# First x loaded by two queues, its statistics raised to the power by halves, and the taps' loads issued by ScalarE

## The chip, the cores and the metric

The kernel runs on one core of a Trainium2 chip. The metric is device time in microseconds (us), the median of the runs of one program. The engines are PE (TensorE: matmuls, with PEld for its weight loads), DVE (VectorE), ACT (ScalarE), POOL (GpSimd) and SP (SyncE, which here only issues transfers). Each engine works through its own instructions in order; a transfer (DMA) is issued by SP, ACT or POOL as one of these instructions and then runs beside them.

## The reference

Two graph layers over 128 graphs of 128 nodes with 256 channels, in float32. Layer 0 is a message-passing layer with a convolution and a GRU; layer 1 is a set of graph convolutions over fixed groups of nodes. Both work on the normalized x:

```python
h = jnp.maximum(_layernorm(x, axis=-1), 0.0)
x = x + _L0_gnn_ref(h, adj, ...)
h = jnp.maximum(_layernorm(x, axis=-1), 0.0)
x = x + _L1_gnn_ref(h, adj, ...)
```

What the change touches is the beginning of layer 0, where `_layernorm(x)` is (x - mean) / sqrt(var + eps) and the convolution branch is:

```python
xc = jnp.transpose(x, (0, 2, 1))
h = _bn(_conv1d(xc, conv1_w, 0), bn1_g, bn1_b, bn1_m, bn1_v)   # 1 tap
h = jax.nn.relu(h)
h = _bn(_conv1d(h, conv2_w, 8), bn2_g, bn2_b, bn2_m, bn2_v)    # 17 taps
x_conv = jnp.transpose(jax.nn.relu(h + xc), (0, 2, 1))
```

`_bn` multiplies by scale = g / sqrt(v + eps) and adds b - m * scale.

## The kernel before

**Tiling.** The 128 graphs are worked in 32 groups q of four graphs, and these in two batches of 16 groups. A group's x is a tile `xa` of 128 partitions by four blocks of 256 channels (512 KB). `load_x` (L385) loads it in four pieces j, one graph each, of 32 partitions and 128 KB; every group's statistics need all four. Four buffers of `xa` are in rotation, so group q uses the buffer of group q - 4, which is free once that one's transposes are done.

**Stage a** (L395), once per group: statistics of the four blocks on DVE (`moments`, L268: bn_stats and bn_aggr for each, then one add of eps), the power -0.5 on POOL (L277, constant `mhalf` out of the tile `cst`), normalizing on DVE (L282), transposes on PE into `ph` (L418), relu on ACT into `hTa` (L420), a store of `hTa` to `hTd` by POOL (L423), the one-tap convolution as matmuls `pc` with `c1w` (L429), the add of the row `brow` on DVE (L432), relu on ACT (L434), and matmuls `pf` that take the result into a Fourier basis (L444), copied into X by DVE and ACT (L450, L452). `hTa` has two buffers: group q waits until the store of group q - 2 has been read out.

**Taps.** The 17-tap convolution is a product in the Fourier basis, so its weights are transformed once, beside stage a: `tap_weights` (L477) goes through four loads n of eight steps m. `load_taps` (L468) brings one load `wt` (two buffers) in five transfers: r = 0 to 3, 256 KB each into 16 partitions, by the issuers passed to it in turn, and the 17th tap (`wt[16::32]`, 64 KB into four partitions) by the first of them. A step is eight matmul instructions `pw` (L496) into four PSUM tiles, three from a pool of three banks (`pgat`) and one from a pool of five (`ptmp`); the copies `ws` (L501 on ACT, L503 on DVE) empty them, ACT two at even m and three at odd m; POOL stores `ws` to `wfd` (L508). Load 0 is issued in `fold`, load 1 before step (n, m) = (0, 3), load 2 before (1, 0) and load 3 before (2, 0). `load_late` (L254) brings three constants (`fus`, `wse`, the rest of `cst`) at step (1, 3).

**The beginning.** `fold` (L285) folds the batch norms: eps is added to both variances on DVE (L292), POOL raises them to -0.5 (L293), `moments` of group 0 follow, then scale and shift of bn1 and bn2, three DVE operations each (L297 to L299). ACT spreads the four columns of bn1's scale and shift into `wide` (L304), PE turns them into rows `prow` (L305), DVE multiplies `c1w` by the scale row (L309) and ACT copies the shift row to `brow` (L310). `normalize` of group 0 stands before that, `brz` (a sum of two GRU biases, needed much later) between.

**Order.** Nothing is reordered after the program text: the generators of the stages are merged by a planner (`Order`, L179) with written costs and due times, which fixes each engine's list. The change leaves costs and due times as they are. At the top, ACT issues the first part of `cst` and `vec` (the bias and batch-norm vectors); SP issues x of group 0, `c1w`, x of groups 1 and 2 (L1235 to L1238), then `fold` runs.

Of the kernel before, what the change touches and what calls it, by code (L numbers as in the profile page):

```python
# [11 lines left out]
ALU = mybir.AluOpType  # L12
# [6 lines left out]
EPS = 1e-5  # L19
# [22 lines left out]
WIDE = 32  # L42
# [104 lines left out]
CFIRST = CAT["tap"][1]  # L147
# [63 lines left out]
def kernel(ctx: ExitStack, tc: tile.TileContext, x, adj, consts, vecs, w_se, conv1_w,  # L211
                    conv2_w, w_msg, b_msg, w_ih, w_hh, W1, W2, b2, fusion_w, out):
    nc = tc.nc
# [16 lines left out]


    cst = cp.tile([P, CONSTS.shape[1]], FP, name="cst")
    nc.scalar.dma_start(out=cst[:, :CFIRST], in_=consts[:, :CFIRST])
    vec = cp.tile([P, NVEC], FP, name="vec")
    nc.scalar.dma_start(out=vec, in_=vecs)

    def c(name):
        a, b = CAT[name]
        return cst[:, a:b]

    def v(name, i=None):
        a, b = VAT[name]
        return vec[:, a:b] if i is None else vec[:, a + i:a + i + 1]
# [10 lines left out]
    def load_late():  # L254

        nc.sync.dma_start(out=fus, in_=fusion_w.partition_broadcast(P))
        nc.sync.dma_start(out=wse, in_=w_se.rearrange("(k p) o -> p k o", p=P))
        nc.sync.dma_start(out=cst[:, CFIRST:], in_=consts[:, CFIRST:])
# [4 lines left out]
    brz = cp.tile([P, 4], FP, name="brz")  # L263
# [4 lines left out]
    def moments(src, tag):  # L268

        st = f2.tile([P, 4, 6], FP, tag=tag + "st", name="st", bufs=4)  # L270
        mv = f2.tile([P, 4, 2], FP, tag=tag + "mv", name="mv", bufs=4)
        rs = f2.tile([P, 4], FP, tag=tag + "rs", name="rs", bufs=4)
        for t in range(4):
            nc.vector.bn_stats(st[:, t], src[:, t])
            nc.vector.bn_aggr(mv[:, t], st[:, t])
        nc.vector.tensor_scalar(rs, mv[:, :, 1], EPS, None, op0=ALU.add)
        nc.gpsimd.tensor_tensor(rs, rs, c("mhalf")[:, :4], ALU.pow)  # L277
        return mv, rs

    def normalize(dst, src, mv, rs):  # L280
        for t in range(4):
            nc.vector.tensor_scalar(dst[:, t], src[:, t], mv[:, t, 0:1], rs[:, t:t + 1],  # L282
                                    op0=ALU.subtract, op1=ALU.mult)

    def fold():  # L285


        s = cp.tile([P, 4], FP, name="s_bn")
        t = cp.tile([P, 4], FP, name="t_bn")
        for i, bn in enumerate(("bn1", "bn2")):  # L290
            scl[bn], sft[bn] = s[:, 2 * i:2 * i + 2], t[:, 2 * i:2 * i + 2]
            nc.vector.tensor_scalar(scl[bn], v(bn + "_v"), EPS, None, op0=ALU.add)  # L292
        nc.gpsimd.tensor_tensor(s, s, c("mhalf")[:, :4], ALU.pow)  # L293
        MOM[0] = moments(XA[0], "a")
        load_taps(0, nc.gpsimd, nc.sync)
        for bn in ("bn1", "bn2"):
            nc.vector.tensor_mul(scl[bn], scl[bn], v(bn + "_g"))  # L297
            nc.vector.tensor_mul(sft[bn], v(bn + "_m"), scl[bn])
            nc.vector.tensor_sub(sft[bn], v(bn + "_b"), sft[bn])  # L299
        prow = ptmp.tile([P, 4, P], FP, tag="tmp", name="prow")  # L300
        wide = tw.tile([P, 4, P], FP, tag="wide", name="wide", bufs=1)
        for i, a in enumerate((scl["bn1"][:, 0:1], scl["bn1"][:, 1:2], sft["bn1"][:, 0:1],
                               sft["bn1"][:, 1:2])):
            nc.scalar.activation(wide[:, i], a.to_broadcast([P, P]), AF.Copy)  # L304
            nc.tensor.matmul(prow[:, i], wide[:, i], ident, start=True, stop=True)  # L305
        normalize(XA[0], XA[0], *MOM[0])
        nc.vector.tensor_add(brz, v("b_ih")[:, 0:4], v("b_hh")[:, 0:4])
        for k in range(2):
            nc.vector.tensor_mul(c1w[:, k], c1w[:, k], prow[:, 0:2].rearrange("p a c -> p (a c)"))  # L309
        nc.scalar.activation(brow, prow[:, 2:4].rearrange("p a c -> p (a c)"), AF.Copy)  # L310

    def fold_gates():

# [61 lines left out]
    LATE, XA, MOM = {}, {}, {}  # L375
# [8 lines left out]

    def load_x(t, q):  # L385
        for j in range(GB):
            nc.sync.dma_start(out=t[j * WIDE:(j + 1) * WIDE],
                              in_=x[q * GB + j].rearrange("(t n) c -> n t c", n=WIDE))

    def load_xa(q):  # L390
        if q not in XA:
            XA[q] = LATE["ab"].tile([P, 4, D], FP, tag="xa", name=f"xa{q}", bufs=4)
            load_x(XA[q], q)
# [74 lines left out]
    def load_taps(n, *engines):  # L468

        wt = tw.tile([P, 16, D], FP, tag="wt", name=f"wt{n}")  # L470
        src = conv2_w.rearrange("(r n i) t o -> n t r i o", r=4, n=4)[n]
        for r in range(4):
            engines[r % len(engines)].dma_start(out=wt[32 * r:32 * r + 16], in_=src[:16, r])
        engines[0].dma_start(out=wt[16::32], in_=src[16])
        wts.append(wt)

    def tap_weights():  # L477

        yield 0.0, 16.0
        for n in range(4):  # L480
            for m in range(8):
                if m == (0 if n else 3) and n < 3:
                    load_taps(n + 1, nc.sync, nc.gpsimd)
                if (n, m) == (1, 3):
                    load_late()
                if (n, m) == (2, 3):
                    nc.scalar.dma_start(out=ad0, in_=adj[:GB].rearrange("b n m -> n b m"))
                    nc.scalar.dma_start(out=bm0, in_=b_msg.partition_broadcast(P))
                if m % 2 == 0:
                    ws = tws[(0, 2, 1)[(4 * n + m // 2) % 3]].tile([P, 4, 4, D], FP, tag="ws",  # L490
                                                                   name=f"ws{n}_{m}")
                pws = [(pgat if r < 3 else ptmp).tile([P, 2, D], FP, tag="gat" if r < 3 else "tmp",
                                                      name=f"pw{n}_{m}_{r}") for r in range(4)]
                for r in range(4):
                    rows = slice(32 * r, 32 * r + TAPS)
                    nc.tensor.matmul(pws[r][:F], c("tap")[rows], wts[n][rows, 2 * m:2 * m + 2],  # L496
                                     start=True, stop=True)
                i = m % 2 * 2
                for r in range(4):
                    if r < 2 or (r == 2 and m % 2):  # L500
                        nc.scalar.activation(ws[:F, r, i:i + 2], pws[r][:F], AF.Copy)  # L501
                    else:
                        nc.vector.tensor_copy(ws[:F, r, i:i + 2], pws[r][:F])  # L503
                yield 0.9, 2.2
                if m % 2:
                    for r in range(4):
                        i0 = 64 * r + 16 * n + 2 * (m - 1)
                        nc.gpsimd.dma_start(out=wfd[:, i0:i0 + 4], in_=ws[:F, r])  # L508
        yield from fold_embedding()
        mid.close()  # L510
        wg = ctx.enter_context(tc.tile_pool(name="wg", bufs=1, reuse_waits="tile"))
        LATE["wrz"] = wg.tile([P, 7, 3, D], FP, name="wrz")
        LATE["wn"] = wg.tile([P, 7, 2, P], FP, name="wn")
        LATE["wh"] = wg.tile([P, 8, 1, P], FP, name="wh")[:, :7]
        LATE["io"] = near.enter_context(tc.tile_pool(name="io", bufs=2, reuse_waits="tile"))
        LATE["xe"] = near.enter_context(tc.tile_pool(name="xe", bufs=1, reuse_waits="tile"))
        LATE["fr"] = near.enter_context(tc.tile_pool(name="fr", bufs=1, reuse_waits="tile"))
        load_h(0)
        LATE["wmsg"] = LATE["fr"].tile([P, 2, D], FP, name="wmsg")
        LATE["bmsg"] = LATE["fr"].tile([P, D], FP, name="bmsg")  # L520
        nc.sync.dma_start(out=LATE["wmsg"], in_=w_msg.rearrange("(k p) o -> p k o", p=P))
        nc.sync.dma_start(out=LATE["bmsg"], in_=b_msg.partition_broadcast(P))
        EN[0] = load_n(0)
# [73 lines left out]
    def load_h(q):  # L597
        HT[q] = LATE["io"].tile([P, 2, 512], FP, tag="hT", name=f"hT{q}")
        nc.sync.dma_start(out=HT[q], in_=hTd[q])

    def load_n(q):
        if q not in HT:
            load_h(q)
        hT = HT.pop(q)
        if q:
            ad = LATE["io"].tile([P, GB, N], FP, tag="adj", name=f"adj{q}")
            nc.sync.dma_start(out=ad, in_=adj[q * GB:(q + 1) * GB].rearrange("b n m -> n b m"))
        return hT, ad if q else ad0
# [624 lines left out]
    order = Order()  # L1233
    take_turn("ab", 2)
    load_xa(0)  # L1235
    nc.sync.dma_start(out=c1w, in_=conv1_w.rearrange("(k p) o -> p k o", p=P))
    load_xa(1)
    load_xa(2)  # L1238
# [68 lines left out]
```

## Time and profile before

| | us |
|---|---|
| median of 3 runs | 1963.19 |
| lowest and highest run | 1960.7, 1964.54 |
| the profiled execution | 1960.66 |
| its span, first to last instruction | 1958.9 |
| PE busy in the span | 1925.5 (98%) |
| DVE, ACT, POOL busy | 1341.2, 670.8, 656.7 |
| share of the chain that ended last: PE, DVE, DMA | 83%, 11%, 2% |

Stage a of the first batch fills the first 155 us, with the taps beside it. In the first 49 us PE is busy for 44.66, in the next 49 for 48.96, in the third 49 for 47.33. The granted clock is 1.00 in all three, and the DMA engines' mean busy share 1.05, 1.03 and 0.89.

A row of the timeline is: start, duration, engine, line, operation, out<-in, count, and in brackets how long the engine stood idle before it and what ended that. The row of a transfer is the issuing instruction's alone ("SPq" and "ACTq" are these engines' own queues); when it landed is seen only by who waited for it. A row of the chain is start, duration and what the end of the kernel hung on in that time.

### The profile page before, as it was taken

The numbers are of one execution on the slowest core, as the hardware profiler recorded it, in microseconds if no ns is written. First come the engines' busy times: TensorE is split into PE (matmuls) and PEld (weight loads), VectorE is DVE, ScalarE is ACT, GpSimd is POOL, SyncE is SP. The second block draws the span as 40 slices with busy tenths as digits, with TensorE's granted clock in tenths as the row PEclk, the third lists the DMA queues.
The fourth block names the chain that finished last, engine by engine and source line by source line (L and its number), as shares of the span: only waits on it lengthen the run. The fifth ranks groups of instructions, "written<-read, shape, count | busy, mean of one in ns | idle before, by whom it ended". The sixth has DMA issues, their size and how long they took to land.

```text
span 1958.9 us, 32171 instructions
## 1 busy us (share of the span) xinstructions
PE 1925.5 (98%) x12048; PEld 1591.1 (81%) x12048; DVE 1341.2 (68%) x2965; ACT 670.8 (34%) x1504; POOL 656.7 (34%) x899
## 2 busy tenths in 40 slices
PE   9999999999999999999999999999999999999997
PEld 6668888889888888887888787888877788887865
DVE  6775445786443576796883886885788787588852
ACT  4664222445223334322223332232332223223233
POOL 3452666332565201332321333231133222114220
PEclk9999999999999999999999999999999999999999
DMA  9988878744778744633433344254344334334232
GB/s 217 308 276 271 272 252 286 218 142 172 251 255 260 213 114 132 188 95 84 112 95 97 96 108 112 79 134 97 92 115 101 89 101 112 100 90 120 63 70 68
DMA packets 180982, 296.66 MB, mean 151 GB/s; under 512 B 28326, under 2 KB 131947, under 8 KB 180571
## 3 DMA queue, kind: packets, MB, share of 16 engines
q1 hardware_dynamic: 134874, 162.20, 28.9%
q0 software_dynamic: 44800, 131.66, 23.8%
q8 instruction: 95, 1.56, 0.3%
q10 hardware_dynamic: 1152, 0.74, 0.1%
q14 instruction: 61, 0.49, 0.1%
HBM read 197.97 MB, written 109.05 MB: 157 GB/s over the span
## 4 chain that ended last, share of the span: by engine, by line
PE 83%; DVE 11%; DMA 2%; ACT 1%; issue 1%; SPq 1%; POOL 0%; DVEq 0%; ACTq 0%; POOLq 0%
PE p L776 37%; PE pa L550 7%; PE pm L663 5%; PE pz L1150 5%; PE ph L1138 5%; PE pc L429 4%; PE pb L550 3%; PE pf L444 3%; PE px L689 3%; PE pi L733 2%; PE pw L496 1%; DMA xa<-in_x 1%; PE ph L418 1%; PE py L1122 1%; DVE xc L742 1%
## 5 line engine op out<-in xcount | busy, mean ns | idle before, releaser
L958 POOL DMA_DIRECT2D x1d<-xt x128 | 101.2, 815 | 403.6 <-DVE xt L956 390.5
L582 DVE SCALAR_TENSOR_TENSOR y<-pa,kk 128x512 f32<-128x512 f32 x78 | 53.8, 690 | 151.4 <-ACT kk L581 151.4
L858 POOL DMA_DIRECT2D xt<-in_x x128 | 100.6, 793 | 161.3 <-DMA x1d<-xt 148.1
L550 PE MATMUL pa<-wf,X 128*128 128x256 f32 x640 | 152.2, 381 | 0.0
L776 PE MATMUL p<-th,wrz 128*128 128x256 f32 x512 | 134.2, 384 | 0.0
L776 PE MATMUL p<-tm,wrz 128*128 128x256 f32 x512 | 131.4, 379 | 0.0
L776 PE MATMUL p<-tc,wrz 128*128 128x256 f32 x512 | 131.4, 379 | 0.0
L550 PEld LDWEIGHTS pa<-wf,X 128*128 128x128 f32 x640 | 118.1, 190 | 16.2 <-issue 2.0
L429 PE MATMUL pc<-c1w,hTa 128*128 128x256 f32 x512 | 120.9, 382 | 2.8 <-DVE X L450 1.7
L663 PE MATMUL pm<-wmsg,hT 128*128 128x256 f32 x512 | 121.5, 382 | 0.0
L776 PEld LDWEIGHTS p<-th,wrz 128*128 128x128 f32 x512 | 94.7, 190 | 19.1 <-issue 6.6
L429 PEld LDWEIGHTS pc<-c1w,hTa 128*128 128x128 f32 x512 | 93.6, 190 | 20.1 <-DVE h L432 4.8
L776 PEld LDWEIGHTS p<-tc,wrz 128*128 128x128 f32 x512 | 97.2, 190 | 13.5 <-issue 0.5
L663 PEld LDWEIGHTS pm<-wmsg,hT 128*128 128x128 f32 x512 | 95.8, 190 | 15.2 <-ACT kk L581 1.4
L776 PEld LDWEIGHTS p<-tm,wrz 128*128 128x128 f32 x512 | 97.3, 190 | 13.2
L745 ACT ACTIVATE xc<-xc,t_bn 128x256 f32<-128x256 f32 x128 | 58.1, 501 | 145.3 <-DVE xc L742 145.3
L776 PE MATMUL p<-hTc,wrz 128*128 128x256 f32 x384 | 99.7, 382 | 1.3 <-DVE z L850 1.2
L776 PE MATMUL p<-xc,wrz 128*128 128x256 f32 x384 | 98.6, 379 | 0.0
L776 PE MATMUL p<-xm,wrz 128*128 128x256 f32 x384 | 98.5, 379 | 0.0
L545 POOL TENSOR_TENSOR wf<-wf 128x512 f32<-128x512 f32 x78 | 98.5, 1263 | 0.0
L1138 PE MATMUL ph<-yz,w 128*128 128x400 f32 (+3 forms) x448 | 96.6, 369 | 1.8 <-DVE yz L1125 1.8
L1150 PE MATMUL pz<-hz,w 128*128 128x400 f32 (+3 forms) x448 | 95.7, 368 | 0.5 <-DVE yz L1152 0.5
(213 smaller groups left out, 4329.5 us busy)
## 6 DMA issues: line engine op xcount, KB each, us to landing
wf<-wfd SPq DMA_DIRECT2D x160, 256.0 KB
wfd<-ws POOLq DMA_DIRECT2D x64, 320.0 KB, 9.3
yd<-y POOLq DMA_DIRECT2D x80, 256.0 KB, 4.4
yt<-yd SPq DMA_DIRECT2D x64, 320.0 KB
xa<-in_x SPq DMA_DIRECT2D x128, 128.0 KB
hTd<-hTa POOLq DMA_DIRECT2D x32, 512.0 KB, 6.5
hT<-hTd SPq DMA_DIRECT2D x32, 512.0 KB
xmd<-xnmp POOLq DMA_DIRECT2D x32, 512.0 KB, 6.0
```

The lines of the kernel that those rows point to most:

```text
L429: nc.tensor.matmul(pc[:, i], hT[:, k, (2 * h + i) * N:(2 * h + i + 1) * N], c1w[:, k], start=(k == 0), stop=(k == 1))
L444: nc.tensor.matmul(pf[:, i, :F * NB], h1[:, 2 * h + i, k * P:(k + 1) * P], fwd, start=True, stop=True)
L545: nc.gpsimd.tensor_tensor(WF[f][:, :, 2], WF[f][:, :, 0], WF[f][:, :, 1], ALU.add)
L550: nc.tensor.matmul(ps, xk(k), WF[f][:, k, s], start=(k == 0), stop=(k == 1))
L663: nc.tensor.matmul(pm[:, i], hT[:, k, j * N:(j + 1) * N], LATE["wmsg"][:, k], start=(k == 0), stop=(k == 1))
L689: nc.tensor.matmul(px[:, dc, i], msgs[h][:, i, dc * P:(dc + 1) * P], aT[:, 2 * h + i], start=True, stop=True)
L745: nc.scalar.activation(xc[:, co, s], xc[:, co, s], AF.Relu, bias=sft["bn2"][:, co:co + 1])
L776: nc.tensor.matmul(ps[:, m], w[:, i, k, m * P:(m + 1) * P], factor(i, x, t), start=first and j == 0, stop=last and j == len(n) - 1, skip_g ...
L858: nc.gpsimd.dma_start(out=xt[a * WIDE:(a + 1) * WIDE].rearrange("p b d c -> p (b d) c"), in_=slices(x[q * GB:(q + 1) * GB])[a])
L958: nc.gpsimd.dma_start(out=slices(x1d[q])[a], in_=xt[a * WIDE:(a + 1) * WIDE].rearrange("p b d c -> p (b d) c"))
L1138: nc.tensor.matmul(ph, w1[:, k, m * P:(m + 1) * P], yz[:, k, s:s + nb, o:o + n], start=(k == 0), stop=(k == 1))
L1150: nc.tensor.matmul(pz, w2[:, g, m, cc * P:(cc + 1) * P], hs[i][:, m], start=(m == 0), stop=(m == 3))
```

## The change

- `cst` and `vec` are no longer issued first by ACT. Pieces 1 and 3 of group 0's x go to ACT, pieces 0 and 2 stay on SP; `cst` follows on ACT, `vec` on SP ahead of `c1w`.
- The moments of group 0 are taken in two halves of two blocks, each with its own add of eps on DVE and its own power on POOL.
- bn2's scale and shift and `brz` come after `c1w` and `brow` instead of before.
- Taps load 0 was issued by POOL (r = 0, 2 and the 17th tap) and SP (r = 1, 3); now by ACT and SP. Loads 1 to 3 were issued by SP (r = 0, 2, 17th tap) and POOL; now by ACT and POOL.

```diff
--- before.py
+++ after.py
@@ -230,9 +230,7 @@
 
 
     cst = cp.tile([P, CONSTS.shape[1]], FP, name="cst")
-    nc.scalar.dma_start(out=cst[:, :CFIRST], in_=consts[:, :CFIRST])
     vec = cp.tile([P, NVEC], FP, name="vec")
-    nc.scalar.dma_start(out=vec, in_=vecs)
 
     def c(name):
         a, b = CAT[name]
@@ -270,11 +268,12 @@
         st = f2.tile([P, 4, 6], FP, tag=tag + "st", name="st", bufs=4)
         mv = f2.tile([P, 4, 2], FP, tag=tag + "mv", name="mv", bufs=4)
         rs = f2.tile([P, 4], FP, tag=tag + "rs", name="rs", bufs=4)
-        for t in range(4):
-            nc.vector.bn_stats(st[:, t], src[:, t])
-            nc.vector.bn_aggr(mv[:, t], st[:, t])
-        nc.vector.tensor_scalar(rs, mv[:, :, 1], EPS, None, op0=ALU.add)
-        nc.gpsimd.tensor_tensor(rs, rs, c("mhalf")[:, :4], ALU.pow)
+        for s in (slice(0, 4),) if src is not XA.get(0) else (slice(0, 2), slice(2, 4)):
+            for t in range(s.start, s.stop):
+                nc.vector.bn_stats(st[:, t], src[:, t])
+                nc.vector.bn_aggr(mv[:, t], st[:, t])
+            nc.vector.tensor_scalar(rs[:, s], mv[:, s, 1], EPS, None, op0=ALU.add)
+            nc.gpsimd.tensor_tensor(rs[:, s], rs[:, s], c("mhalf")[:, s], ALU.pow)
         return mv, rs
 
     def normalize(dst, src, mv, rs):
@@ -292,11 +291,14 @@
             nc.vector.tensor_scalar(scl[bn], v(bn + "_v"), EPS, None, op0=ALU.add)
         nc.gpsimd.tensor_tensor(s, s, c("mhalf")[:, :4], ALU.pow)
         MOM[0] = moments(XA[0], "a")
-        load_taps(0, nc.gpsimd, nc.sync)
-        for bn in ("bn1", "bn2"):
+        load_taps(0, nc.scalar, nc.sync)
+
+        def shift(bn):
             nc.vector.tensor_mul(scl[bn], scl[bn], v(bn + "_g"))
             nc.vector.tensor_mul(sft[bn], v(bn + "_m"), scl[bn])
             nc.vector.tensor_sub(sft[bn], v(bn + "_b"), sft[bn])
+
+        shift("bn1")
         prow = ptmp.tile([P, 4, P], FP, tag="tmp", name="prow")
         wide = tw.tile([P, 4, P], FP, tag="wide", name="wide", bufs=1)
         for i, a in enumerate((scl["bn1"][:, 0:1], scl["bn1"][:, 1:2], sft["bn1"][:, 0:1],
@@ -304,10 +306,11 @@
             nc.scalar.activation(wide[:, i], a.to_broadcast([P, P]), AF.Copy)
             nc.tensor.matmul(prow[:, i], wide[:, i], ident, start=True, stop=True)
         normalize(XA[0], XA[0], *MOM[0])
-        nc.vector.tensor_add(brz, v("b_ih")[:, 0:4], v("b_hh")[:, 0:4])
         for k in range(2):
             nc.vector.tensor_mul(c1w[:, k], c1w[:, k], prow[:, 0:2].rearrange("p a c -> p (a c)"))
         nc.scalar.activation(brow, prow[:, 2:4].rearrange("p a c -> p (a c)"), AF.Copy)
+        shift("bn2")
+        nc.vector.tensor_add(brz, v("b_ih")[:, 0:4], v("b_hh")[:, 0:4])
 
     def fold_gates():
 
@@ -384,7 +387,7 @@
 
     def load_x(t, q):
         for j in range(GB):
-            nc.sync.dma_start(out=t[j * WIDE:(j + 1) * WIDE],
+            (nc.scalar if q == 0 and j % 2 else nc.sync).dma_start(out=t[j * WIDE:(j + 1) * WIDE],
                               in_=x[q * GB + j].rearrange("(t n) c -> n t c", n=WIDE))
 
     def load_xa(q):
@@ -480,7 +483,7 @@
         for n in range(4):
             for m in range(8):
                 if m == (0 if n else 3) and n < 3:
-                    load_taps(n + 1, nc.sync, nc.gpsimd)
+                    load_taps(n + 1, nc.scalar, nc.gpsimd)
                 if (n, m) == (1, 3):
                     load_late()
                 if (n, m) == (2, 3):
@@ -1233,6 +1236,8 @@
     order = Order()
     take_turn("ab", 2)
     load_xa(0)
+    nc.scalar.dma_start(out=cst[:, :CFIRST], in_=consts[:, :CFIRST])
+    nc.sync.dma_start(out=vec, in_=vecs)
     nc.sync.dma_start(out=c1w, in_=conv1_w.rearrange("(k p) o -> p k o", p=P))
     load_xa(1)
     load_xa(2)
```

## The prediction

> **What bounds the kernel now.** I read the page first: PE is busy for 98% of the span, so a change elsewhere counts only where PE stands still for want of it. The chain of waits in order of time says where that is in the part the change touches (start, length, what):
>
> ```profile
> 2.10 3.71 DMA xa<-in_x
> 8.44 1.02 POOL rs L277
> 14.07 1.00 POOL rs L277
> 15.07 12.31 DMA hTd<-hTa
> 28.14 2.05 PE pc L429 x8
> ...
> 98.43 11.71 DMA xa<-in_x
> 113.04 1.99 PE pc L429 x8
> ```
>
> Before 28 us and around 110 us the chain runs through transfers; between and after, it is PE's. The timeline of the first 45 us shows the first stretch:
>
> ```profile
> 8.45 0.51 ACT L304 ACTIVATE wide<-s_bn 128x128 f32<-128x128 f32 x2 [5.51 <-DVE s_bn L297]
> ...
> 9.41 1.35 POOL L473 DMA_DIRECT2D wt<-in_conv_w  x2
> ...
> 10.75 0.66 POOL L474 DMA_DIRECT2D wt<-in_conv_w  x1
> ...
> 25.45 1.18 PE L496 MATMUL pw<-wt,cst 17*80 17x512 f32 x8 [1.11 <-DMA wt<-in_conv_w]
> ...
> 27.49 1.08 ACT L420 ACTIVATE hTa<-ph 128x512 f32<-128x512 f32 x2 [2.38 <-DMA hTd<-hTa]
> ```
>
> PE waits for the first taps; ACT waits until hTa of group 0 has been stored, since group 2 reuses its buffer. The timeline from 74 to 120 us shows the second stretch and the copies that a load on ACT would delay:
>
> ```profile
> 87.08 2.82 SPq L473 DMA_DIRECT2D wt<-in_conv_w  x2
> ...
> 89.94 1.59 SPq L474 DMA_DIRECT2D wt<-in_conv_w  x1
> ...
> 91.64 28.50 SPq L387 DMA_DIRECT2D xa<-in_x  x13
> 91.80 1.06 ACT L501 ACTIVATE ws<-pw 80x512 f32<-80x512 f32 x2
> ...
> 93.93 1.10 PE L496 MATMUL pw<-wt,cst 17*80 17x512 f32 x8
> ...
> 110.16 0.43 DVE L274 BATCH_NORM_STATS2 st<-xa 128x6 f32<-128x256 f32 x1 [2.73 <-DMA xa<-in_x]
> ```
>
> Last, the waits of SP's own queue from 55 to 76 us (who <- for whom: us in total, times, longest):
>
> ```profile
> SPq L473 <- PE pw L496: 14.1, 1, 14.1
> SPq L387 <- DMA wse<-in_w_se: 2.8, 1, 2.8
> SPq L387 <- DMA cst<-in_consts: 2.3, 1, 2.3
> ...
> SPq L258 <- DMA wt<-in_conv_w: 1.6, 1, 1.6
> SPq L257 <- DMA wt<-in_conv_w: 1.3, 1, 1.3
> ```
>
> Two things are in it. SP stands 14.1 us (and 9.8 us before 87.08) for a taps buffer that PE still reads, with the x loads queued behind. And issues wait for earlier transfers that they have nothing to do with. In program order wse (L257) stands eight issues behind the taps' first piece, the rest of cst (L258) eight behind the second, and the last two pieces of x group 10 eight behind wse and cst. In the first 14 us SP also waits 0.4 us for cst, which ACT issued: the second piece of x group 1 stands eight behind it. I read this as **eight transfers in flight, counted over SP and ACT together**; the ninth waits, on its own engine, until the first has landed.
>
> **The start.** Issues of x take 0.45 us each (1.79 for four). With two on each queue the last goes out 0.9 earlier, and cst's 188 KB is no longer ahead of it; vec, third on SP, lands at about 5.0, since it took 3.7 from its issue before. So the moments begin at 5.3, not 5.93. By halves: two pairs of statistics 1.1 and the add 0.2, then a power of 1.0 (POOL's rows with four columns; a narrower one I take as equal) from 6.7 to 7.7; the second half's add ends at 7.9, its power at 8.95. That extra power hides under DVE's second half. bn1's shift is three operations, 0.5, so normalizing starts at 8.4 instead of 9.49 and ends at 9.8: 1.1 us won. bn2's three operations and brz, 0.65 together, come after c1w, ahead of group 1's moments.
>
> But the first taps are now issued by ACT, in program order ahead of `wide` (L304). Their three ACT pieces stand eight behind pieces 0 and 2 of x group 1 and piece 0 of group 2. SP's issues that were freed by the same pieces date these landings: about 7.4, 8.6 and 9.9. The new order feeds taps into the same engines from 7.4 on, so I put the last at 10.4; its issue takes 0.7 (the L474 row), and back-to-back a little more. `wide` then starts at 11.3, not 8.45. Queued behind it on ACT are brow and hTa; DVE waits for prow at c1w and holds group 1's moments: wide to prow 0.9, c1w 0.75, bn2 and brz 0.65, so moments at 13.8 against 11.56. Add 2.4 for them, 1.1 for the power, and normalizing group 1 starts at 17.35, its first transposes on PE at 17.9 against 16.27: **1.6 lost**, the 1.1 included.
>
> From there PE needs 7.0 (16.27 to 23.30) to group 2's transposes, then 1.04, 1.10 and 1.1 for ph, pw and pf: 10.3, where it took 11.9 with both DMA waits. Do these go? The 576 KB of taps leave POOL's queue, where hTd of group 0 stood behind them: 12.3 us to landing against a median of 6.5. It is issued at 17.5 now (after group 1's power), lands by about 24, and is wanted at 27. The taps land before 25 and are wanted at 26.2. So **1.6 won back; the start comes out at 0**. Bounds: `wide` at 10.2, with no extra delay of the landing, gives -1.2; at 13, with every taps packet ahead, +1.5. POOL's 2.0 us of saved issues stood in idle time (its next work was at 14.07) and bring nothing.
>
> A rule speaks against the two queues: the Trainium skill, "DMA: Bandwidth & Descriptors", section "Issuing engines are not separate DMA queues", says that DMAs of all issuers share the same 16 engines and interleave, and that spreading them saves only issue time. By it the first x gains the 0.9 of issue and the store of hTa nothing, which would leave the start at +1.6; the 12.31 row against the 6.5 median speaks for a gain from leaving POOL's queue.
>
> **The later taps loads.** SP no longer stands for the taps' buffer. x group 11 uses the buffer that group 7's transposes free at 75.7, yet went out from 91.64 to 98.43. Now only the in-flight limit holds it: out by about 86, landed well before 107.4, where DVE wants it. The wait of 2.73 goes, and with it 2.7 on PE: pf ended at 111.3 and the next ph began at 116.8 with 2.76 of work between. **-2.7.** Next late would be group 12: its last three pieces stand eight behind taps now issued later. It is wanted at 118.1; I take 0, bound +3.
>
> ACT pays for it. Each load is three issues directly ahead of the copies ws (L501). No row shows them on ACT. SP paid 0.35+1.52+1.24 = 3.1 us (55.21 to 58.4) and 0.36+2.46+1.59 = 4.4 (87.08 to 91.5), both with its own queue empty before; the load at 26.89, spread out by waits, 0.31+0.31+0.70 = 1.3. ACT's two other issues took 0.39 and 0.60 (102.02). Low end 1.3 each; high end 4.65, 4.65 and 6.6, half as much again, since SP's queue is then busy as a third beside POOL's. I take 3.1, 3.1 and 4.4, the rows of the same transfers in the same place. Semaphores cost ACT nothing: the buffer's readers ended before ACT's preceding copies.
>
> What covers it: PE's next pw group needs the banks that ws empties. Load 3: copies end at 92.86, the second matmul pair starts at 94.2: cover 1.35. Load 2: 59.3 and 61.45: 2.15. Load 1 (ws at 38.42, third copy done 39.97, wanted at 41.9): 1.9. PE then loses 3.05, 0.95 and 1.2: **+5.2** (0 to +10.5). PE is the bound in all three places, so nothing returns it. The store of hTd and POOL's wfd stores share the engines with a third queue; I cost that at nothing.
>
> Sum: 0 + 5.2 - 2.7 = +2.5. On the profiled execution, 1960.66 us with a span of 1958.9, this gives 1963.2. That execution lies 2.5 below the median of the runs, 1963.19, and I forecast on the median: **1965.7**, no change as measured (0.2%, 3.9 us, is about what a measurement here can tell from none).
>
> **Rivals.**
> - *Crowded queue, slower.* SP's x loads, no longer held, keep their queue busy when ACT issues; three queues instead of two drain the taps, and the loads cost the high end: 10.5 - 2.7 = +7.8, **1971.0**. It decides once the three loads together take over 12.0 us of ACT (5.4 covered + 2.7 + 3.9); forecast 10.6. For: issues of x at 91.64 to 98.43 took up to 2.57. Against: ACT's 0.39 and 0.60. The skill's "Perfetto Trace Analysis", section "DMA Instruction - HWDGE", has the issuer lock one shared descriptor generator until all descriptors are made, which could add SP's issue to ACT's; no row here shows it, and it would lie on this side.
> - *Cheap issues.* Each load takes under its cover: 0 - 2.7, **1960.5**.
> - *ACT isn't held at the start* (the limit is not shared): 1.1 won at normalizing carries on and the DMA waits go too, -2.7 at the start: 5.2 - 5.4 = -0.2, **1963.0**. The two queues then do what they say.
> - *Both of the last two*: -5.4, **1957.8**.
>
> **Chances.** Forecast 0.44 (its own range 1962 to 1969; 0.06 of it above 1967.1), crowded 0.20, cheap 0.16 (0.02 below 1959.3), not held 0.10, both 0.10 (0.08 below 1959.3). Faster 0.02+0.08 = 0.10; slower 0.06+0.20 = 0.26; the rest, 0.64, the same. The range from 1960.0 to 1971.0 leaves out "both" and half of "crowded".
>
> **What would show it.** ACT's first `wide` near 11.3 with a wait on xa in ACT's own queue (right), or near 8 (not held). Quarter 2's pc near 28.1. ACT's rows of L473 and L474 with their durations: under 2 us a load is "cheap", over 4 "crowded". pw on PE waiting for ACT's ws after each load. No DVE wait for xa near 110. I am wrong outright if PE waits somewhere behind 150 us that it did not wait before.

## The result and the profile after

| | before | after |
|---|---|---|
| median of 5 runs, us | 1961.19 | 1978.19 |
| lowest and highest | 1960.41, 1964.54 | 1974.6, 1978.98 |
| ratio, 95% interval | | 1.0069 (1.0053 to 1.0086) |
| profiled execution, and its span | 1960.66, 1958.9 | 1978.98, 1977.2 |

The change makes the kernel slower by 0.7%; 1965.7 was forecast, and 1978.19 lies above the range. From `load_x` on (L385, now L388) the lines of the changed kernel stand 3 higher: the taps' issues are L476 and L477, ACT's `ws` L504, DVE's L506. Above it they move by other amounts: the power is L276, normalizing L281, `wide` L306.

Engine lines of the two pages, before and after (busy us, share, instructions):

```profile
PE 1925.5 (98%) x12048; PEld 1591.1 (81%) x12048; DVE 1341.2 (68%) x2965; ACT 670.8 (34%) x1504; POOL 656.7 (34%) x899
```

```profile
PE 1936.3 (98%) x12048; PEld 1599.4 (81%) x12048; DVE 1342.4 (68%) x2966; ACT 670.9 (34%) x1504; POOL 653.5 (33%) x897
```

The span grew by 18.3. PE runs the same 12048 instructions and is busy for 10.8 longer; it stands idle only 7.5 longer. So more than half of the loss isn't waiting at all: the same matmuls took longer. The chain of waits of the changed kernel (start, length, what) says where to look:

```profile
4.12 7.72 DMA xa<-in_x
11.86 1.12 ACTq L477
13.01 1.28 ACT L306
14.67 2.09 PE prow L307 x8
...
64.15 7.56 DMA wfd<-ws
72.36 2.48 PE pw L499 x6
74.84 3.71 PE pc L432 x8
```

At the start the chain now runs through ACT: a taps issue that waited for a piece of x, then the activation table load, then `wide`. In the kernel before, the table load stood in idle time:

```profile
1.66 1.28 ACT L304 ACT_TABLE_LOAD   x1 [1.66 <-PEq L1299]
```

Around 70 us it comes off PE, where it was PE's before, and the `pc` behind it takes 3.71 for eight matmuls that took 1.73 elsewhere in the same chain. The timeline there:

```profile
61.73 0.32 ACTq L476 DMA_DIRECT2D wt<-in_conv_w  x1
...
65.34 1.28 DVE L506 COPY ws<-pw 80x512 f32<-80x512 f32 x2 [2.30 <-DMA wfd<-ws]
...
68.11 0.32 ACTq L476 DMA_DIRECT2D wt<-in_conv_w  x1
...
70.96 0.56 ACTq L477 DMA_DIRECT2D wt<-in_conv_w  x1
71.72 1.07 ACT L504 ACTIVATE ws<-pw 80x512 f32<-80x512 f32 x2 [9.07 <-DMA wfd<-ws]
72.36 2.48 PE L499 MATMUL pw<-wt,cst 17*80 17x512 f32 x6 [5.20 <-ACT ws L504]
```

Read it with care: the bracket on ACT's `ws` blames the store of the old `ws`, but DVE writes into the same `ws` tile and could do so at 65.34. The store was done 6.4 before ACT's copy began: the four stores of this buffer, issued from 46.31 on, had landed by 65.22 in the trace, and the store of 64.15, which the chain names, is of a later `ws`. What lies between are ACT's own three issues of load 2: 0.32, 0.32 and 0.56 long, but 6.1 and 2.5 apart. They waited. For what, the trace tells: each transfer of SP or ACT reports its landing on one of eight semaphores, used in turn, and an issue waits for the transfer that had the same one before it. The second issue went out 0.02 after `fus` had landed (68.09), the third 0.02 after `wse` (70.94). SP had issued these two at 52.97 and 56.12; in order of issue over both queues each is the eighth before the one that waits. And PE waited 5.20 for ACT.

The clock over these us (columns: stretch, length, then busy time of PE, PEld, DVE, ACT, POOL, and the granted clock, the DMA share and GB/s):

```profile
64.00:68.00 4.00, 2.71 (x10) 1.31 (x8) 2.66 (x7) 0.00 (x0) 2.54 (x5) 1.00 1.05 367
68.00:72.00 4.00, 0.00 (x0) 0.00 (x0) 0.51 (x1) 0.28 (x1) 1.77 (x4) 0.65 1.04 389
72.00:76.00 4.00, 3.64 (x9) 1.73 (x10) 0.69 (x1) 3.47 (x8) 1.26 (x3) 0.50 1.06 319
76.00:80.00 4.00, 4.00 (x18) 3.19 (x21) 0.69 (x1) 0.68 (x2) 0.82 (x2) 0.57 1.05 281
```

If the clock is either whole or half, 0.65, 0.50 and 0.57 are 2.8, 4.0 and 3.4 us at half: 10.2 together, and PE worked through 7.1 of it (3.64 and 3.4). It falls again in the same way at 14.6 (3.4 us), after load 3 (6.8) and at 383 (3.4; there PE waited 1.16 and 0.47). Before, it stood at 1.00 up to the last few us, although PE waited just as long where the stretch at 383 begins. The rows of that wait, before and after:

```profile
363.69 0.48 PE L676 MATMUL pd<-lr 32*128 32x128 f32 x2 [1.17 <-DVE h L432]
```

```profile
380.84 0.48 PE L679 MATMUL pd<-lr 32*128 32x128 f32 x2 [1.16 <-DVE h L435]
```

So the stretch at 383 has no wait behind it that the change brought. Of the runs below, load3_later and late_by_pool have a stretch there too; wide_first doesn't.

Lag of each group's first `hTa` copy against before, to find the places: +6.2 at group 1, +3.7 at group 2, +4.5 at group 5, +13.8 at group 8 (load 2: 9.3), +19.7 at group 10 (load 3: 5.9), +17.2 at group 12 (x group 11 no longer stalls: -2.6), +18.8 from group 20 (clock at 383: 1.7).

### The profile page after: what moved, and what is told of

Read it like the earlier page. It is cut to its first block, busy times and chain, and to the rows that moved or that the text cites. A ratio compares the mean times of both kernels' runs of the same rounds, so it can differ in the third digit from the quotient of the medians.

```text
span 1977.2 us, 32168 instructions
## 1 busy us (share of the span) xinstructions
PE 1936.3 (98%) x12048; PEld 1599.4 (81%) x12048; DVE 1342.4 (68%) x2966; ACT 670.9 (34%) x1504; POOL 653.5 (33%) x897
## 4 chain that ended last, share of the span: by engine, by line
PE 83%; DVE 11%; DMA 3%; ACT 1%; issue 1%; SPq 0%; POOL 0%; DVEq 0%; ACTq 0%; POOLq 0%
PE p L779 37%; PE pa L553 7%; PE pm L666 5%; PE pz L1153 5%; PE ph L1141 5%; PE pc L432 4%; PE pb L553 3%; PE pf L447 3%; PE px L692 3%; PE pi L736 2%; DMA wfd<-ws 1%; PE pw L499 1%; PE ph L421 1%; PE py L1125 1%; DVE xc L745 1%
## 5 line engine op out<-in xcount | busy, mean ns | idle before, releaser
L779 PEld LDWEIGHTS p<-tc,wrz 128*128 128x128 f32 x512 | 97.3, 190 | 13.5 <-issue 0.5
```

The lines of the kernel that those rows point to most:

```text
L779: nc.tensor.matmul(ps[:, m], w[:, i, k, m * P:(m + 1) * P], factor(i, x, t), start=first and j == 0, stop=last and j == len(n) - 1, skip_g ...
```

## The experiments

The theory after this trace: ACT works in order, so what is queued behind a taps issue waits for whatever that issue waits for, which is an unrelated transfer eight issues back; each time PE then stands, its clock halves for some us. Rivals: the start's own edits carry the loss; SP's x loads, no longer held back, delay POOL's stores of `ws`; the issues themselves are dear on ACT.

Each run was timed beside the kernel before on one chip, in five rounds (before: medians of 1964.13, 1964.07 and 1963.75 in the three groups of runs).

| run | median us | ratio to before | 95% interval |
|---|---|---|---|
| start_only | 1963.8 | 0.9992 | 0.9977 to 1.0008 |
| load0_on_act | 1970.02 | 1.0027 | 1.0013 to 1.004 |
| later_on_act | 1972.15 | 1.0041 | 1.0026 to 1.0055 |
| later_on_pool | 1973.86 | 1.0046 | 1.0031 to 1.0062 |
| late_by_pool | 1964.81 | 1.0009 | 0.9996 to 1.0021 |
| pe_fed | 1968.36 | 1.0022 | 1.0011 to 1.0034 |
| wide_first | 1963.98 | 1.0 | 0.9987 to 1.0012 |
| start_fed | 1963.46 | 1.0006 | 0.9989 to 1.0023 |
| both_repairs | 1965.08 | 1.001 | 1.0 to 1.002 |
| load3_later | 1961.49 | 0.9989 | 0.9975 to 1.0003 |
| before_load3 | 1963.15 | 0.9996 | 0.9982 to 1.001 |
| two_moves | 1961.26 | 0.9995 | 0.9979 to 1.001 |

**start_only**, the change without the taps' new issuer:

```diff
-        load_taps(0, nc.scalar, nc.sync)
+        load_taps(0, nc.gpsimd, nc.sync)
...
-                    load_taps(n + 1, nc.scalar, nc.gpsimd)
+                    load_taps(n + 1, nc.sync, nc.gpsimd)
```

> The changed kernel with all four taps loads issued as before (load 0 by POOL and SP, loads 1 to 3 by SP and POOL). What is left is the first x on two queues, the halves and bn2 later. Theory (the 17 us come from the taps' issues on ACT: +4.7 at the start, 0 at load 1, +10 at load 2, +5 at load 3, -2.5 at x group 11): ACT is not held, so the first wide starts at 8 to 9; cst still lands late (8.4), so POOL's power, and behind it POOL's taps issues, come up to 1.5 later: 1961 to 1963. Rival 1 (the start's own edits carry the loss, because cst and the power come late): +4 or more, 1965 or above. Rival 2 (the two queues do what they say): 1958 to 1960.

0.9992: no difference that can be told. `hTa` of group 0 is 0.85 earlier than before, so these edits together do bring something at the first group; by group 2 it is gone (+0.14), and PE waits 1.60 for the taps, 1.11 before. The start's own edits don't carry the loss: rival 1 falls.

**later_on_act** keeps the second edit of the change alone (load 0 as before), **load0_on_act** the first alone.

> The changed kernel with load 0 alone issued as before, by POOL and SP; loads 1 to 3 stay on ACT and POOL. Theory (losses add up by place): the 4.7 of the start go, 12.5 stay: 1972 to 1975, with the PE wait for ACT's ws at load 2 near 5 us and the PE clock at 0.5 to 0.65 behind it. Rival (load 2's loss is a matter of how the start has shifted the order of transfers, and not of ACT's issues by themselves): load 2 loses 2 us or less, 1963 to 1967.

> The changed kernel with loads 1 to 3 issued as before, by SP and POOL; load 0 stays on ACT and SP. Theory: only the start's 4.7 are left, x group 11 waits again: 1965 to 1967, pc of group 2 near 32.9. Rival (the start's loss is given back later, since PE has other work): 1961 to 1963.

1.0041 and 1.0027. Against start_only that is 0.0049 for the later loads and 0.0035 for load 0; with start_only's -0.0008 they make 1.0076, inside the change's interval. The losses add up by place, and load 2's doesn't hang on the start. In load0_on_act's profile `pc` of group 2 starts at 32.09 in the chain, 4.0 later than before, where 4.7 were expected. The runs lose 5.3 (2.6 to 7.9 by the interval), which fits both. The profiled execution also waited 6.09 near 140 us for a late x piece, which can't be put down to the edit from one look. later_on_act's chain is plainer than the changed kernel's own:

```profile
51.56 15.51 DMA wse<-in_w_se
...
67.09 0.56 ACTq L477
...
67.85 0.60 ACT ws L504
```

ACT's third issue of load 2 waits for the landing of `wse`, 67 KB that SP had issued at 51.56 and that took 15.51. That is the unrelated transfer; the copies into `ws` stand behind it, and PE for 6.32.

**later_on_pool** takes ACT out of the later loads and leaves SP free of them, too:

```diff
-                    load_taps(n + 1, nc.scalar, nc.gpsimd)
+                    load_taps(n + 1, nc.gpsimd)
```

> The changed kernel with loads 1 to 3 issued by POOL alone; load 0 stays on ACT and SP. SP is not kept back by the taps' buffer, as in the changed kernel, but ACT issues none of these loads. Theory (ACT's queue stands at issues that wait for earlier, unrelated transfers): PE's wait for ACT's ws at load 2 goes, load 3's too; +4.7 at the start, -2.5 at x group 11, and up to 3 for POOL's later stores: 1963 to 1967. Rival (SP's x loads, no longer kept back, crowd out the stores of ws, which come free late whoever issues the taps): PE still stands 4 us or more at load 2, stores issued at 46 to 48 land at 62 or later, 1970 to 1976.

The time, 1.0046, lies in the rival's range, but not for the rival's reason. ACT's copies after load 2 start at 62.45, 0.71 after it was free: that is all that waiting for the stores costs there, so crowding by SP's x loads falls as the cause. Of the 0.0046, load 0 on ACT has 0.0027 (load0_on_act); the rest comes from another place (timeline, POOL and DVE):

```profile
80.99 0.51 POOL L511 DMA_DIRECT2D wfd<-ws  x1 [1.87 <-DMA wt<-in_conv_w]
81.52 1.03 POOL L276 TENSOR_TENSOR rs<-rs,cst 128x4 f32<-128x4 f32 x1
82.59 1.38 DVE L281 TENSOR_SCALAR xa<-xa,mv,rs 128x256 f32<-128x256 f32 x4 [7.62 <-POOL rs L276]
```

Now it is POOL's queue that stands: its stores wait for the landing of taps (2.44 at 78.61, 1.87 at 80.99; POOL's transfers have eight semaphores of their own), the power `rs` is queued behind them, DVE waits 7.62 for the power, PE 5.3 for DVE, and the clock is at half for 13.7. Here POOL pays, with what is queued behind these issues. The theory named the wrong price for POOL (up to 3), but its mechanism is the same one.

**late_by_pool** is later_on_act with the three late constants moved off SP, so that load 2 no longer stands eight behind `wse`:

```diff
-        nc.sync.dma_start(out=fus, in_=fusion_w.partition_broadcast(P))
-        nc.sync.dma_start(out=wse, in_=w_se.rearrange("(k p) o -> p k o", p=P))
-        nc.sync.dma_start(out=cst[:, CFIRST:], in_=consts[:, CFIRST:])
+        nc.gpsimd.dma_start(out=fus, in_=fusion_w.partition_broadcast(P))
+        nc.gpsimd.dma_start(out=wse, in_=w_se.rearrange("(k p) o -> p k o", p=P))
+        nc.gpsimd.dma_start(out=cst[:, CFIRST:], in_=consts[:, CFIRST:])
```

> As the run later_on_act (loads 1 to 3 by ACT and POOL, load 0 as before), and the three late constants fus, wse and the rest of cst issued by POOL instead of SP, so that ACT's issues of load 2 no longer stand eight behind fus and wse, but behind pieces of x group 8, which go out some 3 us earlier and are not as slow as wse (15.5 us to landing). Theory (at load 2 ACT is held by the landing of wse, not by the stores of ws and not by the cost of issuing): ACT's ws after load 2 starts by 62 instead of 67.85, PE's wait there falls from 6.3 to under 2, the 0.5 clock behind it goes, and the ratio falls from 1.0041 to 0.998 to 1.001. Rival (the late stores of ws, or the issues by themselves, hold it): PE still waits 4 us or more, ratio 1.003 or above.

As the theory has it: 1.0009. ACT's `ws` starts at 61.15 instead of 67.85, and PE's wait at load 2 goes. ACT still issues the same three transfers there, for 1.93 + 1.41: the issues by themselves cost what the forecast took (3.1), and all but about 0.9 of it hides (`hTa` is 0.3 late at group 5, 1.1 at group 6). In its profile load 3 costs more instead (2.05 + 3.38 on ACT, PE waits 2.63, 6.8 us at half clock), which the other runs show less of.

**pe_fed** is later_on_act with six needless matmuls on PE where it would stand:

```diff
+                if (n, m) == (1, 1):
+                    pfed = ptmp.tile([P, 2, D], FP, tag="tmp", name="pfed")
+                    for _ in range(6):
+                        nc.tensor.matmul(pfed, ident, c1w, start=True, stop=True)
```

> As the run later_on_act, with six matmuls that compute nothing needed put on PE ahead of step (1, 1) of the taps, where PE stood 6.3 us and then ran 10.2 us at half clock. About 0.86 us each, 5.1 together. Theory (the half clock answers to PE's standing still, so half of load 2's loss is clock): the clock stays at 1.00, the next pc takes 1.73 and not 3.71, and some 4 to 5 us come back: 0.998 to 1.0025 against 1.0041. Rival (the clock has fallen for another reason, or the six matmuls cost what they fill): 1.004 or more.

1.0022. ACT is held nearly as long as in later_on_act (`ws` at 66.86 instead of 67.85), yet 3.7 come back at group 7. The same stretches as above, in this kernel:

```profile
64.00:68.00 4.00, 3.86 (x11) 1.20 (x10) 0.00 (x0) 1.14 (x3) 1.16 (x2) 1.00 1.05 400
68.00:72.00 4.00, 4.00 (x26) 2.78 (x28) 1.38 (x2) 2.79 (x7) 2.00 (x4) 1.00 1.08 277
```

The clock stays whole when PE is kept busy. So the half clock answers to PE's standing still, and is a part of the loss that can be had back without touching the wait. By time alone the two runs are hardly apart (their intervals overlap); the clock rows and the 3.7 carry the reading. **start_fed** does the same at the start of load0_on_act, with five more of the idle matmuls that PE begins with:

```diff
-    for _ in range(5):
+    for _ in range(10):
         nc.tensor.matmul(pidle, idle[:, 2, :P], idle[:, :2], start=True, stop=True)
```

> As the run load0_on_act (load 0 by ACT ahead of wide), with ten instead of five idle matmuls at PE's start, so that PE stands about 2 instead of 6.2 us ahead of prow. Theory (half of the start's loss is the clock: 6.8 us at half speed behind the wait): the clock stays at 1.00 in 10 to 20 us and up to 3 us come back, 1.001 to 1.002 against 1.0027. Rival (the clock is not lost to standing still, or what is won there is eaten by the wait for the taps at 25): 1.0025 to 1.003.

1.0006, a little better than expected, with an interval that reaches to 1.0023: the clock is 1.00 from 4 to 20 us, where load0_on_act had 0.50 from 12 to 16; `prow` itself starts only 0.5 earlier (13.42 and 13.90). In time, too, it isn't shown to differ from load0_on_act (1.0013 to 1.004).

**wide_first** is load0_on_act with load 0 moved behind `wide` and `brow` in the program:

```diff
-        load_taps(0, nc.scalar, nc.sync)
...
         nc.scalar.activation(brow, prow[:, 2:4].rearrange("p a c -> p (a c)"), AF.Copy)
+        load_taps(0, nc.scalar, nc.sync)
         shift("bn2")
```

> As the run load0_on_act (only load 0 by ACT and SP), with load 0 issued behind wide and brow instead of ahead of wide. Theory (the start's loss is ACT's queue being held ahead of wide, with the table load and the clock behind it): wide starts at 8.5 to 10, PE's wait of 6.2 falls under 1.5, hTa of group 1 is at 17.4 to 18.5 instead of 23.38; the taps go out some 4 us later and land by 24, just in time; ratio 0.998 to 1.001 against 1.0027. Rival (the taps are then late instead): PE stands 2 us or more for wt near 25 and the ratio stays at 1.002 or above.

1.0, as expected. ACT's first rows of its timeline:

```profile
2.15 1.28 ACT L305 ACT_TABLE_LOAD   x1 [2.15 <-issue]
...
8.64 0.51 ACT L305 ACTIVATE wide<-s_bn 128x128 f32<-128x128 f32 x2 [5.21 <-DVE s_bn L296]
...
11.36 0.82 ACTq L476 DMA_DIRECT2D wt<-in_conv_w  x2
12.21 1.14 ACTq L477 DMA_DIRECT2D wt<-in_conv_w  x1
```

The table load is back in idle time, `wide` starts at 8.64 instead of 13.5 to 14.3, and the issues go out back to back. `hTa` of group 0 now stands behind them (PE waits 2.65), and the taps, issued 9 later than in the changed kernel, are still in time: PE waits for no taps.

**both_repairs** is the whole change with the edits of wide_first and late_by_pool.

> The changed kernel, all four taps loads still issued by ACT, with the two repairs of wide_first and late_by_pool together: load 0 behind wide and brow, and fus, wse and the rest of cst by POOL. Theory (two places where ACT's queue was held make the 17 us, the clock included): the ratios add, 1.0009 from late_by_pool and 0.0008 from wide_first against start_only, so 1.000 to 1.003, 12 us or more under the changed kernel; load 3 may still cost some us. Rival (there is a third loss that the parts did not show): 1.004 or more.

1.001 (1.0 to 1.002), all four loads still issued by ACT. Two places where ACT's queue was held make nearly all of the loss; what is left is of load 3's size (ACT issues for 2.38 + 1.99, PE waits 1.57, 6.8 us at half clock in its profile).

**load3_later**, **before_load3** and **two_moves** look for a faster kernel. The edit, on start_only, on the kernel before, and on wide_first with loads 1 to 3 by SP and POOL:

```diff
-                if m == (0 if n else 3) and n < 3:
+                if n < 3 and m == (3, 0, 2)[n]:
```

> As the run start_only (all taps by the issuers of before), with load 3 issued at step (2, 2) instead of (2, 0): on SP it then stands behind x group 11 instead of ahead of it. Theory (the 2.7 us near 110 us come from x group 11 standing behind SP's wait for the taps' buffer): DVE's wait for xa and PE's 1.66 for X there go, 2.5 us won, ratio 0.9975 to 0.999. Rival (x group 12 or load 3 itself is late next): no gain, 0.999 to 1.002.

> The kernel before with one edit, load 3 at step (2, 2) instead of (2, 0). If the 2.5 us of x group 11 are free for SP's order alone, without the changes of the start: 0.998 to 0.9995. If the gain is lost behind stage a (wmsg): 0.9995 to 1.001.

> wide_first and load3_later together: load 0 by ACT and SP behind wide and brow, loads 1 to 3 by SP and POOL, load 3 at step (2, 2). If the gains add up (wide_first without the DMA waits at 25, load3_later without the stall of x group 11): stage a ends 2 to 3 earlier than before, 0.997 to 0.999. Rival (what stage a gains is given back where wmsg is wanted, PE waited 5.0 for it at 165 in load3_later's profile): 0.9995 to 1.001.

0.9989, 0.9996 and 0.9995, all three with intervals that hold 1: no version is shown to be faster than before. The mechanism is there (against before, group 12 is 1.8 and 2.1 better off than group 10 in load3_later and before_load3). In load3_later's profile it is given back at 165 us, where PE waits for a transfer that it didn't wait for before:

```profile
PE pm L666 <- DMA wmsg<-in_w_msg: 5.0, 1, 5.0
```

The other two don't wait there. before_load3's profile is 0.9 ahead at its last `hTa`, less than the runs can tell; two_moves lost 2.08 waiting for `hTa` near 119 and has two stretches of 3.4 us at half clock.

## Why the prediction was wrong

- **The failed step: "Semaphores cost ACT nothing: the buffer's readers ended before ACT's preceding copies."** It looked at the buffer's semaphores only. The prediction itself had read a limit of eight transfers in flight over SP and ACT, had used it at the start, and had listed `wse` and the rest of `cst` in SP's waits; it didn't ask what stands eight ahead of load 2. Nor would its count have told: it went by program order, where `load_late`, at step (1, 3), comes after load 2. The trace has `fus` and `wse` ahead, since SP had issued them before ACT came to load 2; what fixes the order of the eight isn't shown beyond that it follows the order of issue here. ACT was held there for 9.8 (61.73 to 71.5) where 3.1 was taken, and PE lost 9.3 in place of 0.95. late_by_pool takes this away.
- **The clock was no term of the sum.** 3.4, 10.2, 6.8 and 3.4 us at half, of which PE worked through some 20.6, make about 10.3 of PE's 10.8 extra busy time (an estimate: half of what PE worked at half clock). Each wait of PE was priced at its own length only. pe_fed's and start_fed's clock rows show that the price behind the wait can be had back. 1.7 of it, at 383, is luck: the same waits left the clock whole before.
- **The start: the right mechanism, mis-sized.** ACT was held by landings, as said, but of other transfers: its first taps issue went out at once (2.16), the second waited for `cst` (8.25), and only the third for a piece of x, the second of group 1 (11.84); the prediction, counting in program order, had named three pieces of x. `wide` came at 14.31 and not 11.3: the last piece landed at 11.84 (10.4 taken), the 17th tap's issue took 1.12 (0.7), and the table load, 1.28, had moved behind them, which the prediction missed: it stood at 1.66 before, in idle time, and goes where ACT's first activation is in ACT's order. `cst`, third on ACT instead of first, held the power until 8.39, so normalizing began at 10.15 and not 8.4. (The prediction's own terms put group 1's moments at 13.6, not 13.8; they began at 18.01.) The DMA waits went, as said (2.5 won back between groups 1 and 2). Taken: 0; measured: 4.5, the clock's share in it.
- **Load 1: taken 1.2, measured 0.** The issues took 2.0 (41.82 to 43.9) and were covered.
- **Load 3: taken 3.05, measured 5.9**, 6.8 us at half clock behind a PE wait of only 1.2. ACT's issues took 4.0 (4.4 was taken), with no wait among them: here the price was the issues' own. From run to run they took between 1.5 (later_on_act) and 5.4 (late_by_pool); what sets that was not tried.
- **x group 11: -2.7 taken, -2.6 measured.** Right.
- **The skill's rule on shared engines** that the prediction weighed ("DMA: Bandwidth & Descriptors", "Issuing engines are not separate DMA queues": several issuers save issue time alone). Of the 0.9 of issue, little reached the kernel: in start_only the moments begin at 5.70 instead of 5.93, held by `vec` (5.52). The rest of group 0's 0.85 comes with the halves: normalizing begins at 8.75 instead of 9.49, although the last add of eps ends at the same 8.35. The rule doesn't give what came between groups 1 and 2: in wide_first `hTa` is 1.4 late at group 1 and 1.1 early at group 2, without the waits for taps and for the store, which landed 7.6 after its issue and not 12.3. That leaving POOL's queue did this is likely but not shown alone, since the taps also went out at other times.
- **Stores at nothing:** the stores of `ws` issued near 47 did land 16.7 later, but PE waited only 0.45 for that (DVE's copies at 65.34). Nearly right.
- **The rivals.** "ACT isn't held at the start" and "cheap issues" fall. "Crowded queue" named the right side and a point of decision, 12.0 us of ACT, that was passed (15.9 over the three loads); but its mechanism, dear issues, isn't what happened at load 2, where most was lost: its issue rows are 0.32 to 0.56 long, the rest is waiting.

## What to carry to other kernels

A transfer's issue is an instruction of an engine that works in order: before it is given to an engine that computes, list what it must wait for, the limit on transfers in flight included and at every place where it is issued, and what is queued behind it. Count that limit in the order in which the issues go out, which here was not program order. SP, with only transfers behind it, stood 14.1 us at an issue and 9.8 at the next (for the taps' buffer), for 2.7 of loss in all; ACT, held for 9.8, and POOL, held for 2.44 and 1.87, each cost PE more than 5. And a wait of the engine that bounds the kernel is to be priced with the clock behind it: in the profiled execution that was some 10 of 18.3 us.

## What the runs showed of the hardware

- PE's clock fell to half in stretches of 3.4 us or multiples (3.4, 6.8, 10.2, 13.7), after waits of PE of 5.0 to 6.3, and went back to whole some us after PE was busy again. Of shorter waits some had this behind them (1.2 at load 3: 6.8) and some not (1.67 near 113 in the kernel before, 2.65 in wide_first). Waits of 1.17 and 0.47 at the same place had it in the changed kernel and not in the one before.
- The Trainium skill, "TensorE: Matmul & The Clock Gate", Part 1, "What's actually happening", has the clock halve after an idle window of about 3.4 us and come back after a busy one, the windows running freely. The unit and the halving agree with these traces; 6.8 us at half behind a wait of 1.2 is more than that section alone would give.
- 67 KB (`wse`) took 15.51 us to land in later_on_act, where the DMA share stood at 1.02 to 1.05 throughout. With the engines that full, its size said little of when it would land.
